# A conv, attention and expert block on one core: token loads two pieces ahead, delta products on VectorE, other ring sizes

## The chip, the cores and the metric

The kernel runs on one core of a Trainium2 chip. A core has five engines, each with its own queue that is worked in order: TensorE (PE, matmuls, results in PSUM), VectorE (DVE), ScalarE (ACT, activation functions), GpSimd (POOL) and SyncE (SP, here only for issuing DMAs). They meet through semaphores. All data comes from HBM by DMA into SBUF, 128 partitions wide. The metric is device time in microseconds (us) of one execution; lower is better.

## The reference

`x` is four images of 64 x 64 tokens with 128 channels, in float32. Layer 0 normalises each image in groups of 4 channels and adds the output of a selective-scan block; layer 1 adds an attention block and then an expert block, each on normalised tokens.

```python
x = x + _L0_conv_ref(_gn(x), ...)                 # scan block
t = _to_tokens(x)
t = t + _L1_attn_ref(_ln_t(t), ...)               # 16 heads of width 8
t = t + _L1_ffn_ref(_ln_t(t), ...)                # 64 experts, top 8 tokens for each
```

What matters here is the scan block. Each image's 4096 tokens are scanned in three orders: forward, backward, and in 16 interleaved slices. For each order:

```python
x = silu(causal_conv1d(x, conv_w, conv_b))                 # 256 rows, 4 taps
x_dbl = einsum('rd,bdl->brl', x_proj_w, x)                 # 8 rows of dt, 16 of B, 16 of C
delta = softplus(einsum('dr,brl->bdl', dt_w, dt_raw) + dt_b)
# for each token:  h = h * exp(delta * A) + (delta * u) * B ;  y = sum over 16 states of h * C
y = (y + D * x) * silu(z)
```

The three results are added and projected back to 128 channels.

## The kernel before

The program has an opening stage and three later ones. In the opening stage the scan inputs of all four images are made, and image 0 is scanned. Then comes a short stretch that prepares image 0 for the attention, then the attention loops of the four images with the scans of images 1 to 3 and other work running beside them, then the experts. The change touches the opening stage alone.

**Pieces and their order.** The code is written as Python generators. Each `yield` is a place where another generator may go on; the order in which instructions are recorded is the order in each engine's queue, and nothing reorders it afterwards. In `tile_kernel` (L1532 to L1541) two such streams are woven: `first` is the scan of image 0, `others` makes the inputs of all images. Each turn `others` takes 1.3 yields on average and `first` takes one. Within `others`, `flow` keeps two pieces active. So the number of yields in a piece decides how its instructions stand against the scan's.

**Inputs.** `norm` (L288) reads one image. In four pieces of 1024 tokens it loads tokens into `x_g` (512 KB, SP, one buffer), transposes them on PE in two halves of four 128 x 128 blocks, copies each half to `xn` (ACT, L308) and takes `bn_stats` of it (DVE, L311). The statistics are then combined over groups with two tiny matmuls, and `xn` is scaled in place (DVE, L332). `of_chunk` (L369) makes, for one image, order and chunk of 1024 tokens: the convolution on PE, `u` by silu on ACT, the projections, and `r` = delta by softplus on ACT (L431). `u`, `r` and the rows of B and C are stored to DRAM (SP). For "early" chunks, all 12 of image 0 and the first two of image 1, `of_chunk` also multiplies delta by u, in place in `u`, two products of 128 x 1024 (L440), and stores that as `d_du`; the very first chunk does so on DVE, the other 13 on POOL. The u that is overwritten must have been stored first. Later chunks get that product elsewhere, beside the attention. `gate` makes silu(z).

**Scan of image 0.** `of_image` (L475) with `alone=True` runs 384 steps: 3 orders, 4 chunks, 32 steps each. A step covers 16 rows times 8 states on 128 partitions and 1024 tokens. For each step:

- `load` (L501), four steps ahead: delta (SP queue) and du (ACT queue), 512 KB each for two steps, spread from DRAM over the partitions; three buffers of delta and four of du. At a chunk's start also the B and C rows, in two halves `q` (L487). Half 0 comes from a ring of three buffers in the pool `rows`, half 1 from two in the pool `lone`.
- `exp` (L521), three steps ahead: dA = exp(A delta) on ACT. The first step of a pair writes a tile of its own, the second overwrites delta.
- `inputs` (L530), one step ahead: dB = du x B on DVE (L537), written to PSUM.
- `step` (L539): the scan itself, one `tensor_tensor_scan` on DVE (L547); the chunk's last column is kept by a small POOL copy (`ends`, L549, not in an order's last chunk); then POOL multiplies h by C into `hC` (L554), a ring of five tiles.
- `sums`/`total`: PE adds up over the states (L585, `y`), for two steps at a time, one block of four steps later. This frees the tiles of `hC`.
- `out`: once per four steps DVE adds D u (L601), and SP stores the result.

So DVE's queue repeats scan, dB, scan, dB, with the occasional instruction of `others` behind a dB, and POOL's repeats ends, hC. In the very first chunk SP also issues 96 small loads of A (L231), once image 0's norm is recorded.

Of the kernel before, what the change touches and what calls it, by code (L numbers as in the profile page):

```python
# [11 lines left out]
F32 = mybir.dt.float32  # L12
# [4 lines left out]
P = 128  # L17
C = 128
# [8 lines left out]
T = 1024  # L27
# [184 lines left out]
def orders(b):  # L212

    return ORDERS[min(b, 1)]
# [20 lines left out]
class Inputs:  # L235
# [52 lines left out]
    def norm(self, b):  # L288

        nc = self.nc  # L290
        while b - 1 in self.gated and self.gated[b - 1] < NC:
            yield WAIT
        self.gated[b] = 0
        xin = self.x[b].rearrange("(t p) c -> p t c", p=P)
        xn = self.big.tile([P, L + 6], F32, tag="xn", name=f"xn_{b}")
        nc.gpsimd.memset(xn[:, 0:3], 0.0)
        nc.gpsimd.memset(xn[:, L + 3 :], 0.0)
        stats = self.small.tile([P, L // 512, 6], F32, tag="stats", name=f"stats_{b}")
        for g in range(NC):
            x_g = self.piece.tile([P, 8, C], F32, tag="x_g", name=f"x_{b}_{g}")  # L300
            nc.sync.dma_start(out=x_g, in_=xin[:, g * 8 : g * 8 + 8, :])
            yield
            for k in range(2):
                ps = yield from self.bank(f"xt_{b}_{g}_{k}")
                for i in range(4):
                    nc.tensor.transpose(ps[:, i * P : (i + 1) * P], x_g[:, 4 * k + i, :], self.ident)
                cut = xn[:, 3 + g * T + k * 512 : 3 + g * T + (k + 1) * 512]
                nc.scalar.copy(cut, ps)  # L308
                self.leave()
                yield  # L310
                nc.vector.bn_stats(stats[:, 2 * g + k, :], cut)  # L311
        mv = self.small.tile([P, 2], F32, tag="mv", name=f"mv_{b}")
        nc.vector.bn_aggr(mv, stats.rearrange("p g s -> p (g s)"))
        gm = self.small.tile([P, 4], F32, tag="gm", name=f"gms_{b}")
        ps = yield from self.bank(f"gm_{b}")
        nc.tensor.matmul(ps[:, 0:1], self.group, mv[:, 0:1], start=True, stop=True)
        yield
        nc.vector.tensor_copy(gm[:, 0:1], ps[:, 0:1])
        self.leave()
        nc.vector.tensor_sub(gm[:, 1:2], mv[:, 0:1], gm[:, 0:1])  # L320
        nc.vector.tensor_mul(gm[:, 1:2], gm[:, 1:2], gm[:, 1:2])
        nc.vector.tensor_add(gm[:, 1:2], gm[:, 1:2], mv[:, 1:2])
        ps = yield from self.bank(f"gv_{b}")
        nc.tensor.matmul(ps[:, 0:1], self.group, gm[:, 1:2], start=True, stop=True)
        yield
        nc.vector.tensor_copy(gm[:, 2:3], ps[:, 0:1])
        self.leave()
        rstd_of(nc, gm[:, 3:4], gm[:, 2:3], *self.cols)
        yield
        for g in range(NC):  # L330
            cut = xn[:, 3 + g * T : 3 + (g + 1) * T]
            nc.vector.tensor_scalar(cut, cut, gm[:, 0:1], gm[:, 3:4], ALU.subtract, ALU.mult)  # L332
        self.normed[b] = xn
# [35 lines left out]
    def of_chunk(self, b, order, c):  # L369
        while b not in self.normed or (order == 2 and b not in self.sliced):  # L370
            yield WAIT
        src = self.sliced[b] if order == 2 else self.normed[b]
        nc, w, key = self.nc, self.ws[order], f"{b}_{order}_{c}"
        made = {
            "delta": self.dram.tile([DI, T], F32, name=f"d_delta_{key}"),
            "du": self.dram.tile([DI, T], F32, name=f"d_du_{key}"),
            "u": self.dram.tile([DI, T], F32, name=f"d_u_{key}"),
            "bc": self.dram.tile([2, NS, T], F32, name=f"d_bc_{key}"),
        }

        def keep(name, t):
            nc.sync.dma_start(out=made[name].rearrange("(m p) t -> p m t", p=P), in_=t)

        def reads(k, g):

            at = c * T + g * 512
            if order == 1:
                end = L + 6 - at - k
                return src[:, end - 512 : end][:, ::-1]
            return src[:, at + k : at + k + 512]  # L390

        halves = [slice(g * 512, (g + 1) * 512) for g in range(T // 512)]
        u = self.piece.tile([P, 2, T], F32, tag="u", bufs=2, name=f"u_{key}")
        banks = yield from self.banks(4, f"cv_{key}")
        for m in range(2):
            for g in range(2):
                for k in range(4):
                    nc.tensor.matmul(  # L398
                        banks[2 * m + g], w["conv"][:, k, m * P : (m + 1) * P], reads(k, g), start=(k == 0), stop=(k == 3)
                    )  # L400
                yield
        yield
        for m in range(2):
            for g, cut in enumerate(halves):
                nc.scalar.activation(u[:, m, cut], banks[2 * m + g], AF.Silu, bias=w["conv_b"][:, m : m + 1])
                self.leave()
        yield
        xd = self.piece.tile([X_ROWS, T], F32, tag="xd", name=f"xds_{key}")
        for g, cut in enumerate(halves):
            ps = yield from self.bank(f"xd_{key}_{g}")  # L410
            for m in range(2):
                nc.tensor.matmul(ps[:X_ROWS], w["x"][:, m, :], u[:, m, cut], start=(m == 0), stop=(m == 1))  # L412
            yield
            nc.scalar.copy(xd[:, cut], ps[:X_ROWS])
            self.leave()
        keep("u", u)
        yield
        r = self.piece.tile([P, 2, T], F32, tag="r", name=f"r_{key}")
        banks = yield from self.banks(4, f"dt_{key}")
        for m in range(2):  # L420
            for g, cut in enumerate(halves):
                at = 32 * (2 * m + g)
                rows = slice(at, at + R)
                nc.tensor.matmul(banks[2 * m + g], w["dt"][rows, m, :], xd[rows, cut], start=True, stop=True)
        nc.sync.dma_start(out=made["bc"][0], in_=xd[B_ROW : B_ROW + NS])
        nc.sync.dma_start(out=made["bc"][1], in_=xd[C_ROW : C_ROW + NS])
        yield
        yield
        for m in range(2):
            for g, cut in enumerate(halves):  # L430
                nc.scalar.activation(  # L431
                    r[:, m, cut], banks[2 * m + g], AF.Softplus, bias=w["dt_proj_b"][:, m : m + 1]
                )
                self.leave()
        yield
        by_early = early(b, order, c)
        if by_early:
            by = nc.vector if (b, order, c) == (0, orders(0)[0], 0) else nc.gpsimd
            for m in range(2):
                by.tensor_mul(u[:, m, :], r[:, m, :], u[:, m, :])  # L440
        yield
        keep("delta", r)
        if by_early:
            yield
            keep("du", u)
        self.made[b, order, c] = made
        yield


class Scans:  # L450
# [24 lines left out]
    def of_image(self, b, made, alone=False):  # L475
# [10 lines left out]

        def rows_of(order, c, q):  # L487
            for i, name in enumerate(("B", "C")):
                if alone and q:
                    t = self.lone.tile([P, T], F32, tag=name, bufs=2, name=f"{name}{q}_{b}_{order}_{c}")  # L490
                else:
                    t = self.rows.tile([P, T], F32, tag=name, bufs=3, name=f"{name}{q}_{b}_{order}_{c}")
                src = made[b, order, c]["bc"][i, q * NS2 : (q + 1) * NS2]
                nc.sync.dma_start(out=t, in_=src.unsqueeze(0).to_broadcast([16, NS2, T]))
                spread[order, c, name, q] = t
            if q == 1:
                return
            if c < NC - 1:
                ends[order, c] = self.small.tile([P, NB], F32, tag="ends", name=f"ends_{b}_{order}_{c}")
# [39 lines left out]
        def step(s):  # L539
# [10 lines left out]
            if alone:  # L550
                if s + 1 < n:
                    inputs(s + 1)
                tiles["du", s] = self.lone.tile([P, T], F32, tag="hC", bufs=5, name=f"hC_{b}_{s}")
                nc.gpsimd.tensor_mul(tiles["du", s], h, spread[order, c, "C", j % 2])  # L554
                return
            if s + 1 < n:
# [951 lines left out]
def tile_kernel(tc, ctx, x, in_proj_w, dirs, out_proj_w, attn, gate, weight1, weight2, out):  # L1508
# [15 lines left out]
    with ExitStack() as fill:  # L1524
# [10 lines left out]
        with tc.manual_schedule():  # L1535
            first = Pace(decays(nc, dirs, ws, inputs), scans.of_image(0, inputs.made, True))
            others = Pace(flow(inputs.pieces(range(nb)), 2, 10))
            while not first.done:
                others.run(1.3)
                first.run(1.0)  # L1540
            others.rest()  # L1541
    bank = scans.bank = Bank(ctx.enter_context(tc.tile_pool(name="bank", bufs=1, space=PSUM)), 1)
# [115 lines left out]
```

## Time and profile before

The times of four runs are 11401.74 to 11427.02 us, median 11415.23 us. The profiled execution is one more:

| | |
|---|---|
| profiled execution, its own time | 11421.51 us |
| its span | 11419.8 us |
| granted TensorE clock, mean | 0.943 |
| busy: PE, DVE, ACT, POOL | 86%, 73%, 87%, 33% |
| first scan of image 0 starts | 107.0 us |
| last scan of image 0 ends | 1815.5 us |
| busy from 0 to 1816 us: PE, DVE, ACT, POOL | 1350, 1601, 1091, 1352 us |
| first exponential of the attention starts | 2061.1 us |
| last one starts | 11168.4 us |

How to read it: "busy" is the time in which an engine had an instruction at work. A row of the groups gives line, engine, operation, tiles out and in, their sizes and the count; then the busy time and the mean of one in ns; then the idle time of the engine just before them and what ended it. A row of a timeline gives start, duration, engine, line and operation, and in brackets the idle time before it with its releaser. The chain of waits is the work that ended last, followed back from the end.

### The profile page before, as it was taken

The numbers are of one execution on the slowest core, as the hardware profiler recorded it, in microseconds if no ns is written. First come the engines' busy times: TensorE is split into PE (matmuls) and PEld (weight loads), VectorE is DVE, ScalarE is ACT, GpSimd is POOL, SyncE is SP. The second block draws the span as 40 slices with busy tenths as digits, with TensorE's granted clock in tenths as the row PEclk, the third lists the DMA queues.
The fourth block names the chain that finished last, engine by engine and source line by source line (L and its number), as shares of the span: only waits on it lengthen the run. The fifth ranks groups of instructions, "written<-read, shape, count | busy, mean of one in ns | idle before, by whom it ended". The sixth has DMA issues, their size and how long they took to land.

```text
span 11419.8 us, 183032 instructions
## 1 busy us (share of the span) xinstructions
PE 9875.4 (86%) x68358; PEld 3271.3 (29%) x68358; DVE 8315.2 (73%) x8379; ACT 9990.0 (87%) x10828; POOL 3800.4 (33%) x3917
## 2 busy tenths in 40 slices
PE   6787782788988889899998898999998999999995
PEld 2233331222222222222222222222222223333323
DVE  7998897888988987999988979988999321111212
ACT  4566572899999999999999999999999999989992
POOL 5887674332323213424233224233332110000000
PEclk8898895899999999999999999999999999999997
DMA  6787796555565665655656755655556332222225
GB/s 191 226 243 227 216 245 191 161 147 152 148 155 152 179 170 153 157 152 141 154 145 160 193 155 154 158 144 146 146 150 164 116 100 72 76 71 84 75 65 186
DMA packets 900979, 1747.51 MB, mean 153 GB/s; under 512 B 203150, under 2 KB 443846, under 8 KB 899830
## 3 DMA queue, kind: packets, MB, share of 16 engines
q1 hardware_dynamic: 764734, 1469.68, 47.4%
q0 software_dynamic: 93856, 156.41, 4.9%
q10 hardware_dynamic: 41496, 109.71, 3.6%
q8 instruction: 537, 8.80, 0.3%
q14 instruction: 356, 2.92, 0.1%
HBM read 1379.76 MB, written 355.47 MB: 152 GB/s over the span
## 4 chain that ended last, share of the span: by engine, by line
PE 37%; ACT 23%; DVE 14%; issue 14%; DMA 9%; SPq 1%; POOL 1%; ACTq 0%; DVEq 0%; POOLq 0%
PE acc L998 21%; ACT e L989 19%; PE s L984 10%; DVE h L547 6%; DMA delta<-d_delta 3%; DVE dB L537 2%; DMA du<-d_du 2%; PE cv L398 1%; ACT dA L528 1%; PE y L585 1%; ACT delta L528 1%; PE fo L1155 1%; PE h L1142 1%; DMA x<-in_x_dram 1%; PE xd L412 1%
## 5 line engine op out<-in xcount | busy, mean ns | idle before, releaser
L989 ACT ACTIVATE e<-s 128x1024 f32<-128x1024 f32 x8192 | 7773.9, 1105 | 233.7 <-PE s L984 222.2
L998 PE MATMUL acc<-e,val 128*32 128x512 f32 x32768 | 5253.7, 616 | 105.8 <-ACT av L1007 93.1
L984 PE MATMUL s<-qm,key 32*128 32x512 f32 x16384 | 2646.9, 501 | 591.6 <-ACT e L989 559.9
L984 PEld LDWEIGHTS s<-qm,key 32*128 32x128 f32 x16384 | 1012.1, 184 | 4451.9 <-issue 2495.1
L549 POOL COPY ends<-h 128x1 f32<-128x1 f32 x1152 | 1284.3, 1116 | 2282.3 <-DVE h L547 2274.8
L537 DVE TENSOR_TENSOR dB<-du,B 128x1024 f32<-128x1024 f32 x960 | 1301.1, 1355 | 428.9 <-PE y L585 224.7
L998 PEld LDWEIGHTS acc<-e,val 128*32 128x32 f32 x32768 | 971.6, 109 | 1606.5 <-issue 789.0
L547 DVE TENSOR_TENSOR_SCAN h<-dA,ends,dB 128x1024 f32<-128x1024 f32 x576 | 1350.4, 2344 | 101.7 <-ACT dA L528 59.0
L528 ACT ACTIVATE dA<-delta,A 128x1024 f32<-128x1024 f32 x768 | 935.6, 1218 | 462.0 <-DMA delta<-d_delta 429.2
L547 DVE TENSOR_TENSOR_SCAN h<-delta,ends,du 128x1024 f32<-128x1024 f32 x432 | 1012.3, 2343 | 126.0 <-ACT delta L528 64.0
L554 POOL TENSOR_TENSOR hC<-h,C 128x1024 f32<-128x1024 f32 x384 | 985.4, 2567 | 209.4 <-PE y L585 108.8
L528 ACT ACTIVATE delta<-delta,A 128x1024 f32<-128x1024 f32 x768 | 936.9, 1220 | 6.3 <-ACT dA L528 0.8
L558 DVE TENSOR_TENSOR du<-h,C 128x1024 f32<-128x1024 f32 x576 | 701.1, 1217 | 0.1
L558 DVE TENSOR_TENSOR dB<-h,C 128x1024 f32<-128x1024 f32 x576 | 701.0, 1217 | 0.0
L537 DVE TENSOR_TENSOR du<-du,B 128x1024 f32<-128x1024 f32 x576 | 690.5, 1199 | 4.5 <-DMA B<-d_bc 4.4
L1013 POOL DMA_DIRECT2D d_ctx<-av x512 | 260.2, 518 | 1015.3 <-DVE av L1007 645.8
L398 PE MATMUL cv<-xn,conv 128*128 128x512 f32 x1024 | 478.8, 622 | 38.1 <-DVE xn L332 25.8
L579 POOL DMA_DIRECT2D d_du<-x_delta x272 | 157.2, 578 | 1015.4 <-DVE x_delta L578 954.7
L547 DVE TENSOR_TENSOR_SCAN h<-dA,dB 128x1024 f32<-128x1024 f32 x192 | 438.8, 2285 | 43.4 <-ACT dA L528 32.4
L585 PE MATMUL y<-dB,sel 128*32 128x256 f32 x4608 | 376.8, 399 | 7.6 <-DVE xT L1182 5.0
L547 DVE TENSOR_TENSOR_SCAN h<-delta,du 128x1024 f32<-128x1024 f32 x144 | 328.9, 2284 | 67.4 <-issue 34.6
L585 PE MATMUL y<-du,sel 128*32 128x256 f32 x4608 | 361.9, 386 | 0.0
(246 smaller groups left out, 7115.5 us busy)
## 6 DMA issues: line engine op xcount, KB each, us to landing
delta<-d_delta SPq DMA_DIRECT2D x768, 512.0 KB
du<-d_du SPq DMA_DIRECT2D x576, 512.0 KB
du<-d_du ACTq DMA_DIRECT2D x192, 512.0 KB
key<-d_q SPq DMA_DIRECT2D x352, 256.0 KB
d_u<-u SPq DMA_DIRECT2D x48, 1024.0 KB
d_delta<-r SPq DMA_DIRECT2D x48, 1024.0 KB
B<-d_bc SPq DMA_DIRECT2D x96, 512.0 KB
C<-d_bc SPq DMA_DIRECT2D x96, 512.0 KB
```

Source lines behind the costliest of these rows:

```text
L398: nc.tensor.matmul(banks[2 * m + g], w["conv"][:, k, m * P : (m + 1) * P], reads(k, g), start=(k == 0), stop=(k == 3))
L528: nc.scalar.activation(tiles["delta", s], t, AF.Exp, scale=A)
L537: nc.vector.tensor_mul(tiles["du", s], du, spread[order, c, "B", j % 2])
L547: nc.vector.tensor_tensor_scan(h, dA, dB, first, ALU.mult, ALU.add)
L549: nc.gpsimd.tensor_copy(ends[order, c][:, at : at + 1], h[:, T - 1 :])
L554: nc.gpsimd.tensor_mul(tiles["du", s], h, spread[order, c, "C", j % 2])
L558: nc.vector.tensor_mul(dB, h, spread[order, c, "C", j % 2])
L585: nc.tensor.matmul(y[32 * g : 32 * g + 32, : T // 4], self.sel[:, j // 2, :], hC[:, 256 * g : 256 * g + 256], start=(j == 0), stop=(j == 3),)
L984: nc.tensor.matmul(s_ps[:, k, :], keys[f"{i // 4}"][rows, cut].bitcast(F32R), queries[j, qb][rows, :].bitcast(F32R), start=True, stop=True,)
L989: nc.scalar.activation(e, s_ps, AF.Exp, scale=1.0 / math.sqrt(D))
L998: nc.tensor.matmul(accs[j, qb][32 * k : 32 * k + 32, :], v[:, k * VW : k * VW + 32], es[i][k // 2][:, k % 2, :], start=(kc == 0), stop=(kc ...
L1013: nc.gpsimd.dma_start(out=self.context[b][h * D : h * D + D, cut], in_=av[32 * k : 32 * k + D, :])
```

## The change

There are five edits, all in the opening stage.

1. `norm`: `x_g` gets two buffers. The first two loads are recorded at once, with six yields after them (one for image 0); the load of piece g + 2 is recorded after piece g. Each `bn_stats` is recorded after the copy two halves later, with a yield of its own; the last two follow at the end.
2. `of_chunk`: the delta products of all early chunks are recorded on DVE, each with a yield behind it.
3. `rows_of`: for image 0, three of every four tiles of B and of C come from `rows`, and each fourth (half 1 of an odd chunk) from `lone`, where one tile is left of each.
4. `step`: `hC` has six tiles.
5. `tile_kernel`: `others` takes 1.4 yields a turn.

The second `x_g` buffer and the sixth `hC` tile take 4 KB of each partition, each; the two dropped tiles of B and C give back 8 KB.

```diff
@@ norm
+        def bring(g):
+            x_g = self.piece.tile([P, 8, C], F32, tag="x_g", bufs=2, name=f"x_{b}_{g}")
+            nc.sync.dma_start(out=x_g, in_=xin[:, g * 8 : g * 8 + 8, :])
+            return x_g
+
+        coming, made = [bring(0), bring(1)], []
+        for _ in range(6 if b else 1):
+            yield
         for g in range(NC):
-            x_g = self.piece.tile([P, 8, C], F32, tag="x_g", name=f"x_{b}_{g}")
-            nc.sync.dma_start(out=x_g, in_=xin[:, g * 8 : g * 8 + 8, :])
-            yield
+            x_g = coming[g]
             for k in range(2):
...
                 nc.scalar.copy(cut, ps)
                 self.leave()
+                made.append(cut)
                 yield
-                nc.vector.bn_stats(stats[:, 2 * g + k, :], cut)
+                if len(made) > 2:
+                    nc.vector.bn_stats(stats[:, len(made) - 3, :], made[-3])
+                    yield
+            if g + 2 < NC:
+                coming.append(bring(g + 2))
+        for i in range(len(made) - 2, len(made)):
+            nc.vector.bn_stats(stats[:, i, :], made[i])
+            yield
@@ of_chunk
         if by_early:
-            by = nc.vector if (b, order, c) == (0, orders(0)[0], 0) else nc.gpsimd
             for m in range(2):
-                by.tensor_mul(u[:, m, :], r[:, m, :], u[:, m, :])
+                nc.vector.tensor_mul(u[:, m, :], r[:, m, :], u[:, m, :])
+                yield
@@ rows_of
-                if alone and q:
-                    t = self.lone.tile([P, T], F32, tag=name, bufs=2, name=...)
+                if alone and 2 * (c % 2) + q == 3:
+                    t = self.lone.tile([P, T], F32, tag=name, name=...)
@@ step
-                tiles["du", s] = self.lone.tile([P, T], F32, tag="hC", bufs=5, name=f"hC_{b}_{s}")
+                tiles["du", s] = self.lone.tile([P, T], F32, tag="hC", bufs=6, name=f"hC_{b}_{s}")
@@ tile_kernel
-                others.run(1.3)
+                others.run(1.4)
```

More of the change, by code (lines that the diff above doesn't have):

```diff
@@ L488, in rows_of @@
             for i, name in enumerate(("B", "C")):
-                if alone and q:
-                    t = self.lone.tile([P, T], F32, tag=name, bufs=2, name=f"{name}{q}_{b}_{order}_{c}")
+                if alone and 2 * (c % 2) + q == 3:
+                    t = self.lone.tile([P, T], F32, tag=name, name=f"{name}{q}_{b}_{order}_{c}")
                 else:
```

## Prediction

> **What bounds the kernel now.** I read the page's slices first (where is which engine full), then the groups of instructions and the waits of the first 1816 us, then the timelines of VectorE and GpSimd there. Slices:
>
> ```profile
> PE   6787782788988889899998898999998999999995
> DVE  7998897888988987999988979988999321111212
> ACT  4566572899999999999999999999999999989992
> POOL 5887674332323213424233224233332110000000
> ```
>
> A slice is 285 us. In the first six, DVE and POOL are full and ACT is not; afterwards ACT and PE are (attention). Everything the change touches lies in the opening stage: the scan of image 0 ends at 1815.5 us, and the attention opens only on its stored result. Later instructions are the same on every engine, so what the opening gains or loses passes on whole. Its groups on DVE, from the first scan on:
>
> ```profile
> L537 DVE TENSOR_TENSOR dB<-du,B 128x1024 f32<-128x1024 f32 x383 | 604.4, 1578 | 23.5 <-DMA du<-d_du 9.5 <-DMA B<-d_bc 1.2
> L547 DVE TENSOR_TENSOR_SCAN h<-dA,ends,dB 128x1024 f32<-128x1024 f32 x144 | 337.8, 2346 | 20.9 <-ACT dA L528 3.8
> L311 DVE BATCH_NORM_STATS2 stats<-xn 128x6 f32<-128x512 f32 x24 | 16.6, 691 | 52.1 <-ACT xn L308 52.0
> ...
> L440 POOL TENSOR_TENSOR u<-r,u 128x1024 f32<-128x1024 f32 x26 | 72.4, 2805 | 8.6 <-ACT r L431 8.6
> ```
>
> Two things are to be seen. DVE's one large wait is that of the statistics for ScalarE's copy: 52.0 us. And dB takes 1578 ns in the mean, where an undisturbed one takes 1.23 us. The timelines say why:
>
> ```profile
> 326.94 5.59 POOL L440 TENSOR_TENSOR u<-r,u 128x1024 f32<-128x1024 f32 x2 [0.51 <-ACT r L431]
> 332.48 1.18 POOL L549 COPY ends<-h 128x1 f32<-128x1 f32 x1
> 333.62 2.36 POOL L554 TENSOR_TENSOR hC<-h,C 128x1024 f32<-128x1024 f32 x1
> ...
> 328.13 2.35 DVE L547 TENSOR_TENSOR_SCAN h<-dA,ends,dB 128x1024 f32<-128x1024 f32 x1
> 330.51 3.11 DVE L537 TENSOR_TENSOR dB<-du,B 128x1024 f32<-128x1024 f32 x1
> 333.75 2.35 DVE L547 TENSOR_TENSOR_SCAN h<-delta,ends,dB 128x1024 f32<-128x1024 f32 x1
> 336.13 3.38 DVE L537 TENSOR_TENSOR dB<-du,B 128x1024 f32<-128x1024 f32 x1
> ```
>
> A scan and a POOL product run side by side, but a product of DVE and one of POOL exclude each other: dB, begun at 330.51 while POOL works, ends with POOL's u. In phase, hC hides under the scan (2.35 beside 2.35 us) and dB costs 1.23; whatever delays POOL pushes hC onto the next dB, at up to 2.2 us each. Summed over the opening's dBs, what exceeds 1.24 us is 132 us. Going back on POOL from each: 54 us (28 dBs) follow an L440 product, 75 us (50 dBs) an hC that waited for its buffer, thus for PE's y (POOL's waits: "PE y L585" 108.8 us, and six at the start of a chunk, 58.9 us, put down to "issue", where y was late too). Such a wait:
>
> ```profile
> 1117.86 2.48 POOL L554 TENSOR_TENSOR hC<-h,C 128x1024 f32<-128x1024 f32 x1 [3.44 <-PE y L585]
> ...
> 1120.65 3.23 DVE L537 TENSOR_TENSOR dB<-du,B 128x1024 f32<-128x1024 f32 x1
> ```
>
> **The change part by part**
>
> *Start of image 0: -11 us.* With one x_g buffer the four loads go in turn; image 0's statistics wait 4.8 us before each later piece and the last ends at 53.2 us. With two buffers, pieces 0 and 1 are there when PE becomes free at 30.8; loads 2 and 3 are issued at about 32.5 and 33.5 instead of 39 and 45.5, and land 4.3 us later (their length in the chain), with both and the A loads in flight perhaps 6: the last statistics end near 42. SP, which issues 96 small A loads (37 us) behind the last x load and only then lets the first u out (82.76), also comes 11-12 us earlier, so neither holds the other back. Bounds: 0 (x_1, now ahead of the dt weights on SP, delays weight work that ends at 30.8) and -16.9 (all of image 0's waits of the statistics).
>
> *Norms of images 1 to 3: -39 us.* The waits are 20.3, 16.8 and 14.9 us (at 465, 890 and 1300 us): a bn_stats stands right behind its copy, the copy behind a transpose, that behind a load that waited for the only buffer. Now the first two loads go out some two scan steps (8 us) ahead, the third and fourth about three steps before their copies, and each bn_stats stands two copies later. ScalarE's exp leads the scan by a median of 7 to 8 us, so a copy that waits 1 to 3 us for its load is mostly absorbed there; what would be late next is exp, and the scan behind it. I leave a quarter of the 52. Bounds -52 and 0. SP gains nothing in issues (16 loads of 0.38 us either way) but waits less in front of delta loads: it stood 36.8 us for "PE xt" and 35.8 us for earlier x loads.
>
> *Six tiles for hC, ring of four for B and C: -44 us.* y is summed for two steps at a time, one block later, so with five tiles step 4k+5 reuses the tile of step 4k, whose y is issued in that same step: no slack. With six the tightest reuse has one step, 3.7 us. Most of POOL's gaps for y are 0.8 to 3.6 us and vanish; eight of 4.0 to 6.4 leave 0.3 to 2.7 (together 9 us), the six at chunk starts (6.5 to 12.9) leave about 22. 75 - 31 = 44. Bounds 0 and -75. B and C cost nothing: in either ring a tile is reloaded when its chunk of two before has ended, four steps ahead of need.
>
> *Delta products on DVE: +45 us.* Off: the 54 us above. On: 26 products of 1.18 us (the pair that DVE does already takes 2.36): 30.7. The wait: each product stands in DVE's queue for r, the softplus on ScalarE, one yield behind it, while ScalarE issues one or two steps ahead of DVE. For each of the 13 chunks I took from the trace the end of the exp ahead of its softplus plus 1.28 (table load) and 1.24 (two halves), and the end of the dB before the product: 2.2, 2.1, 6.1, 4.8, 3.7, 4.8, 0.9, 5.0, 9.3, 0, 4.4, 0.6, 0: 44 us. Behind the waiting product stands the scan, and behind that delta's buffers, so ScalarE cannot run ahead meanwhile. In numbers, chunk (1,2): DVE would come to the product at 292.9, when ScalarE has this still ahead of it:
>
> ```profile
> 294.01 1.15 ACT L528 ACTIVATE dA<-delta,A 128x1024 f32<-128x1024 f32 x1 [1.43 <-DMA delta<-d_delta]
> 295.17 1.28 ACT L431 ACT_TABLE_LOAD   x1
> 296.47 0.69 ACT L431 ACTIVATE r<-dt,dt_proj_b 128x512 f32<-128x512 f32 x1
> ```
>
> Last, the port: what follows a dB at once and needs two SBUF streams loses its turn to the waiting ends copy and hC. Three of three first xn scalings (L332) show it: 2.97 us for 0.80, +2.17:
>
> ```profile
> 530.08 5.14 DVE L332 TENSOR_SCALAR xn<-xn,gms 128x1024 f32<-128x1024 f32 x4
> ...
> 530.17 2.33 POOL L554 TENSOR_TENSOR hC<-h,C 128x1024 f32<-128x1024 f32 x1
> ```
>
> A first product that waits longer hides this; the six that wait less pay 7.4 more. In eight chunks the new yield puts the second product behind the next dB: 8 x 2.17 = 17.4. Sum 30.7 + 44 + 7.4 + 17.4 - 54 = +45. Bounds: -23 (no waits, no lost turns) and +90 (waits twice as long). A delta product also waits for the store of u that it overwrites (26.9 us in image 0's first chunk, where SP is behind the A loads); no later one on POOL did, so I take nothing.
>
> The Trainium skill (Perfetto Trace Analysis, Optimizing Scalar/DVE Operations) says that because the two engines share a read port, moving work between them might not help. By that rule alone this part would be 0 and the whole sum -84 instead of -39; the rows above decide, since they price DVE's new wait for r, of which the rule says nothing.
>
> *Pace 1.4: 0.* Yields grow by 10 or 5 per norm and 2 in each of 14 chunks, 63 on some 880 (7%), the rate by 7.7%; the last softplus comes 4 steps later of 384, with 19 steps of plain scanning left to cover it.
>
> *Returned: +10.* Three delta pairs circulate: a load is issued when a scan frees its buffer, its exp starts 7 to 13 us later, and is used five scans after the issue. Shorter steps shorten that lead. DVE's waits for exp, du and B are 39 us now; a quarter more is 10 (bounds 0 and +39).
>
> Sum: -11 - 39 - 44 + 45 + 10 = -39 us. The profiled execution took 11421.5 us (span 11419.8), 6.3 above the median of 11415.2, an ordinary run; against the median this gives **11376 us**.
>
> **Rivals**
>
> *Slower: the wait for r.* One mechanism, in the 13 early chunks (110 to 600 us). Against it stand exps that end before the scan needs them; for it stand ScalarE's waits for delta (298.1 us in 63 waits), which come ahead of softplus in its queue. Without the waits the sum is -39 - 44 = -83. It decides once they total 83 us, 6.4 a chunk (two of the 13 estimates are near or above that); at 106 us, 8.2 a chunk (the largest estimate is 9.3), the time is 11415 + 23 = 11438.
>
> *Nothing from the norms.* The copies still stand in ScalarE's queue: if the loads stay late, exp is late and the scan waits where bn_stats did. 11376 + 39 = 11415. For it: one copy waited 15.2 us for its transpose; against it: the load now leaves two to three steps ahead.
>
> *hC keeps colliding.* If PE's y is late by more than a step, the sixth tile moves the gap by one step and no more: 11376 + 44 = 11420. For it: the chunk-start gaps of up to 12.9 us; against it: 3.6 us or less in most.
>
> *Delta products free.* If DVE finds r ready and POOL's order does not shift, that part is -23 to 0: 11308 to 11331. For it: three estimates near 0.
>
> **How the numbers follow.** The median of four runs spreads 25 us, so less than 0.2% (23 us) can't be told from no change. Forecast (11345 to 11392) 0.42; delta products free, below 11345, 0.22; nothing from the norms or from hC, 11392 to 11438, 0.18; slower 0.18. Faster by over 0.2%: 0.64. Eight in ten: 11295 (all gains near their bounds) to 11445 (slower case, its nearer half).
>
> **What would show it.** Right: the scan of image 0 ends near 1776 instead of 1815.5; "stats <- ACT xn" falls from 52 to some 13 us after the start; the first scan begins near 96 instead of 107; dB's mean goes from 1578 towards 1330 ns; POOL's "PE y" waits halve; and a new DVE wait "u <- ACT r" of some 44 us appears, with u's mean near 2.1 us instead of 1.18. Wrong: if that wait exceeds 100 us, if the wait of the statistics returns as "h <- ACT delta", or if the attention, from 1815 us on, does not just shift.

## The result, and the profile after

The changed kernel takes 11402.05 us (median of 34 runs) against 11412.03 us for the kernel before (52 runs): a ratio of 0.9991, with an interval of 0.9987 to 0.9996. That is 10 us, or 0.09%: clear of zero, but below the 0.2% under which the prediction counted no change. The forecast was 11376 us; its range of 11295 to 11445 holds the result.

The profiled execution has a span of 11399.4 us (own time 11401.1 us), 20.4 less than before's 11419.8. First DVE's and POOL's slices of the page after, as shown for before:

```profile
DVE  6889898888888987999988979988998221111212
POOL 5778784332323212424233124233331110000000
```

The picture is the old one: in the first six slices DVE and POOL are both full. DVE stands a tenth lower in the first three; POOL stands a tenth lower in the second and third, and a tenth higher in the three after them. The groups of VectorE from the first scan to the last scan of image 0, after (busy us, mean ns, idle us ahead):

```profile
L551 DVE TENSOR_TENSOR dB<-du,B 128x1024 f32<-128x1024 f32 x384 | 517.0, 1346 | 40.5 <-DMA du<-d_du 23.2 <-DMA B<-d_bc 4.8
L453 DVE TENSOR_TENSOR u<-r,u 128x1024 f32<-128x1024 f32 x26 | 37.8, 1468 | 57.9 <-ACT r L445 40.0 <-DMA du<-d_du 14.6 <-DMA d_u<-u 3.3
```

dB fell from 1578 to 1346 ns, as foretold (1330). In its place stands a new group, the delta products: 37.8 us of work and 57.9 us of waiting. VectorE's waits, in us, times and the longest, first after, then before:

```profile
DVE h L561 <- ACT dA L542: 23.8, 21, 3.2
DVE dB L551 <- DMA du<-d_du: 23.2, 13, 6.9
DVE h L561 <- ACT delta L542: 20.5, 15, 2.5
DVE stats L319 <- ACT xn L314: 19.1, 4, 9.6
```

```profile
DVE dB L537 <- DMA du<-d_du: 16.3, 6, 6.8
DVE h L547 <- ACT delta L528: 13.1, 6, 2.6
DVE h L547 <- ACT dA L528: 8.7, 9, 2.4
```

The statistics wait 19.1 us instead of 52.0, but the scan now waits 44.3 us for its exponentials instead of 21.8, and dB 23.2 for du instead of 16.3 (some 7 us of either lie ahead of the first scan).

The traces of this study were cut in the same way. "Excess" is what the dBs take beyond 1.24 us each; "other waits" is all idle time of VectorE between the first and the last scan of image 0 that is not the statistics' or the delta products'. In us, from one profiled execution of each kernel:

| kernel | first scan | last scan ends | excess of dB | products: work + wait | statistics wait | other waits | first exp of attention, after last scan |
|---|---|---|---|---|---|---|---|
| before | 107.0 | 1815.5 | 131.5 | on POOL | 52.1 | 85.3 | 245.6 |
| after | 98.5 | 1808.4 | 43.4 | 38.2 + 57.9 | 19.1 | 116.3 | 242.4 |
| e1_products_pool | 99.5 | 1777.8 | 94.1 | on POOL | 19.9 | 126.7 | 242.8 |
| e2_products_alone | 107.4 | 1819.6 | 63.7 | 47.3 + 34.5 | 59.5 | 74.3 | 244.4 |
| e3_norm_alone | 99.2 | 1739.1 | 123.1 | on POOL | 13.2 | 74.6 | 251.5 |
| e4_six_alone | 108.0 | 1809.1 | 94.2 | on POOL | 54.7 | 112.6 | 245.9 |
| e5_pace13 | 99.3 | 1779.8 | 33.1 | 41.4 + 54.6 | 19.5 | 100.8 | 275.2 |
| e6_products_later | 98.4 | 1765.5 | 48.5 | 49.4 + 14.2 | 12.6 | 108.8 | 244.2 |
| e7_delta4 | 99.4 | 1745.0 | 134.5 | on POOL | 13.8 | 68.4 | 251.1 |
| e8_norm_six | 99.1 | 1723.7 | 94.3 | on POOL | 14.8 | 86.4 | 252.7 |
| e9_norm_pace14 | 99.5 | 1799.3 | 164.3 | on POOL | 6.2 | 94.3 | 243.8 |
| e10_norm_products | 98.6 | 1744.3 | 73.1 | 48.2 + 13.1 | 10.8 | 74.1 | 250.6 |
| e11_norm_products_six | 99.7 | 1726.4 | 37.0 | 49.1 + 11.1 | 13.1 | 89.9 | 253.2 |
| e12_norm_pace135 | 99.9 | 1755.4 | 135.1 | on POOL | 12.2 | 72.6 | 244.0 |

From before to after the scan of image 0 ends 7.1 us earlier: start -8.5, excess -88.1, products +96.1, statistics -33.0, other waits +31.0, the rest -4.6. Of the 20.4 us of the span, 12.4 lie in the attention loops (first to last exponential: 9108.4 and 9096.0 us). All fourteen traces here have 9096 to 9119 us there with the same instructions, so that part is put down to the spread of single executions (the 52 runs of before span 33 us); the runs say 10 us.

### The profile page after: what moved, and what is told of

Same layout as the page of the kernel before. It is cut to its first block, busy times and chain, and to the rows that moved or that the text cites. A ratio compares the mean times of both kernels' runs of the same rounds, so it can differ in the third digit from the quotient of the medians.

```text
span 11399.4 us, 183033 instructions
## 1 busy us (share of the span) xinstructions
PE 9874.8 (87%) x68358; PEld 3271.9 (29%) x68358; DVE 8259.6 (72%) x8405; ACT 9988.6 (88%) x10828; POOL 3744.8 (33%) x3891
## 4 chain that ended last, share of the span: by engine, by line
PE 37%; ACT 24%; issue 14%; DVE 13%; DMA 10%; POOL 1%; SPq 1%; ACTq 0%; DVEq 0%; POOLq 0%
PE acc L1012 21%; ACT e L1003 20%; PE s L998 10%; DVE h L561 6%; DMA delta<-d_delta 4%; PE cv L412 2%; DVE dB L551 2%; DMA du<-d_du 1%; ACT dA L542 1%; ACT delta L542 1%; PE y L599 1%; PE fo L1169 1%; PE h L1156 1%; PE xd L426 1%; DVE du L572 1%
## 5 line engine op out<-in xcount | busy, mean ns | idle before, releaser
L551 DVE TENSOR_TENSOR dB<-du,B 128x1024 f32<-128x1024 f32 x960 | 1212.6, 1263 | 422.2 <-PE y L599 219.1
L568 POOL TENSOR_TENSOR hC<-h,C 128x1024 f32<-128x1024 f32 x384 | 993.4, 2587 | 166.1 <-PE y L599 85.9
L599 PE MATMUL y<-hC,sel 128*32 128x256 f32 x3072 | 246.4, 454 | 166.1 <-DVE o L615 154.0
```

The costliest lines, as they stand in the source:

```text
L551: nc.vector.tensor_mul(tiles["du", s], du, spread[order, c, "B", j % 2])
L599: nc.tensor.matmul(y[32 * g : 32 * g + 32, : T // 4], self.sel[:, j // 2, :], hC[:, 256 * g : 256 * g + 256], start=(j == 0), stop=(j == 3),)
```

## The experiments

**First: each part by itself, and the pace.** The theory was the sum of the prediction: gains at the norms and the six tiles, a price for the delta products behind the softplus, nothing for the pace. The main rival was that removed waits come back as other waits. e1 to e4 ran on one chip beside the kernel before (median there 11424.49 us). e5, e6, e7 and e9 ran on a second (11423.73 us), e8, e10, e11 and e12 on a third (11420.42 us). So kernels are compared by their ratios.

*e1_products_pool* is the change with the products back on POOL, its two yields kept.

```diff
-                nc.vector.tensor_mul(u[:, m, :], r[:, m, :], u[:, m, :])
+                by.tensor_mul(u[:, m, :], r[:, m, :], u[:, m, :])
```

> The changed kernel with the delta products of the 13 early chunks back on POOL (their yields stay). Theory 'price on DVE': in the changed kernel the 26 products cost DVE 38 us of work and 58 us of waits in front of them, against 54 us of collisions that they caused on POOL. Taking them off DVE then gives 96 - 54 = 42 us, less some 15 us that shorter steps give back as waits for exp: about 11375 us, with the wait 'u <- ACT r' gone from DVE, dB's excess back from 43 to about 95 us, and the scan stretch (first to last scan of image 0) near 1680 us instead of 1710. Rival 'the move pays': the collisions come back in full, with those by late y in chunks 0 to 3 (68 us in the kernel before): 11440 us or more. Rival 'floor': the loop of delta loads bounds the opening, so that what DVE gains comes back as waits for exp: 11395 to 11410 us.

Measured: 11381.83 us, 0.9961 (0.9948 to 0.9973). The products' move costs the changed kernel 0.30%, some 34 us, near what the theory said; in the traces the scan of image 0 ends 30.6 us later with them on DVE. The prediction said +45.

*e2_products_alone* is the kernel before with only the products moved to DVE, with their yields, at pace 1.3.

```diff
-                by.tensor_mul(u[:, m, :], r[:, m, :], u[:, m, :])
+                nc.vector.tensor_mul(u[:, m, :], r[:, m, :], u[:, m, :])
+                yield
```

> The kernel before with the delta products on DVE and their yields, and nothing else of the change (pace 1.3, one x_g buffer, five hC tiles). Theory 'price on DVE': +42 us, 11454 us, slower than before by 0.3 to 0.5%. Rival 'the move pays': 11412 us or less. Rival 'floor': the waits for r lie beside waits for exp that are there anyway: 11405 to 11425 us.

Measured: 11424.71 us, 0.9999 (0.9990 to 1.0008). Not as the theory had it: here the move is free to within 10 us. dB's mean falls to 1399 ns, and against that stands the new wait (VectorE's waits):

```profile
DVE u L439 <- ACT r L431: 34.4, 8, 7.3
```

The excess falls by 67.8 us where 54 were taken to go, and the wait is 34.4 us where 44 were taken; work and wait are 81.8 us. The statistics wait 7.4 us longer, and other waits are 11.0 us shorter. The time is the one that the rival 'floor' named (11405 to 11425 us); its reason, that the waits for r lie beside waits that are there anyway, holds for those 11 us. So the price of the move isn't one number. That it depends on how far ScalarE is behind when DVE reaches the product is argued here; e6 tests it.

*e3_norm_alone* has the norm part alone: two `x_g` buffers, loads ahead, later statistics. Room for the buffer comes from the ring of B and C, which has the change's form; `hC` has five tiles, the products are on POOL, the pace is 1.3.

```diff
+        coming, made = [bring(0), bring(1)], []
...
+                    nc.vector.bn_stats(stats[:, len(made) - 3, :], made[-3])
...
+                if alone and 2 * (c % 2) + q == 3:
```

> The kernel before with the two x_g buffers, the early loads and the late statistics (the ring of four for B and C makes the room), products on POOL, five hC tiles, pace 1.3. Theory: -8 us at the start and -33 us in three norms, 11371 us; the wait of the statistics after the first scan falls from 52 to about 19 us. Rival 'floor': 11395 us or more, with 'h <- ACT' up by what the statistics lose.

Measured: 11359.21 us, 0.9943 (0.9930 to 0.9955), a gain of 65 us: more than the expectation, and more than six times that of the whole change. VectorE's waits there: the statistics stand at 13.2 us, as the prediction had it, and nothing came back: the scan's waits for exponentials (10.0 us, and 3.2 for those that overwrite delta) are together below the 21.8 us of before.

```profile
DVE stats L319 <- ACT xn L314: 13.2, 3, 7.5
DVE h L561 <- ACT dA L542: 10.0, 8, 2.5
```

One thing goes with this part unasked: its yields (10 or 5 a norm, 35 in all) slow the pieces. Their last gate matmul ends when the scan is at step 383 of 384; before it was step 361. No run separates that from the loads and the statistics, nor the ring of B and C from either; e9 and e12 bear on it.

*e4_six_alone* is the kernel before with the six tiles and the other ring of B and C.

```diff
-                tiles["du", s] = self.lone.tile([P, T], F32, tag="hC", bufs=5, name=f"hC_{b}_{s}")
+                tiles["du", s] = self.lone.tile([P, T], F32, tag="hC", bufs=6, name=f"hC_{b}_{s}")
```

> The kernel before with six hC tiles and the ring of four for B and C, nothing else. Theory: the dB excess that late y caused, 75 us, falls to about 31 us, so -44 us, less 10 to 15 us of waits for exp: about 11380 us. Rival 'floor': 11400 us or more, with dB's excess down and the waits for exp and du up by nearly as much. Rival 'y is late by more than a step': dB's excess hardly falls, 11410 us.

Measured: 11416.01 us, 0.9991 (0.9983 to 1.0000). POOL's waits for y halve and the excess falls by 37.3 us, near the 44 of the prediction. But 27.3 us come back as other waits of DVE, above all for exponentials (24.6 us and, for those that overwrite delta, 15.3). From the waits of POOL and of VectorE (before, POOL's were 108.8 us and this one of VectorE's 8.7):

```profile
POOL hC L554 <- PE y L585: 58.0, 24, 6.7
```

```profile
DVE h L547 <- ACT dA L528: 24.6, 17, 3.2
```

Here the rival holds: POOL no longer holds DVE up, and DVE then meets the next late thing. Of the 37.3 us, 29.3 lie in the last eight chunks of the scan, and so does all that came back. Whether one late moment of PE and ScalarE had delayed both is not shown.

*e5_pace13* is the change at the old pace.

```diff
-                others.run(1.4)
+                others.run(1.3)
```

> The changed kernel with the pace of 1.3 instead of 1.4. What is left open by the first four runs: six hC tiles took 37 us of dB excess away and got 27 us of waits for exp and du back; the changed kernel has 116 us of them, the two norms alone at pace 1.3 only 75. Theory 'pace': 1.4 puts 7.7% more of the other pieces' work into ScalarE's queue per scan step, ahead of the exps; at 1.3 those waits fall from 116 towards 85 us, and 20 to 30 us are gained in the scan, less what the inputs cost that then remain when the scan ends (63 yields more at the old pace: some 9 steps' worth of pieces after the last scan, 5 to 20 us): 11375 to 11395 us. Theory 'tiles': the waits for exp come from shorter steps, the pace does nothing: 11400 us or, with the remainder, 11410.

Measured: 11416.99 us, 0.9996 (0.9987 to 1.0004). The scan of image 0 ends 28.6 us earlier, as theory 'pace' had it, but the first exponential of the attention stands 275.2 us behind it instead of 242.4: the last gate matmul of the pieces ends at 1805.1 us, 25 us after the scan. This remainder had been put at 5 to 20 us; it is 33 us and takes back all that the scan gained, so the time is not the one expected. With the added yields in the pieces, 1.3 is too slow to finish them; 1.4 finishes them, and costs the scan as much.

**Second: where the loss of the change lies.** The parts alone add up to 0.57% + 0.09% + 0.01%, some 76 us, and together they gave 10.

*e6_products_later* is the change with the delta products two yields later, behind the store of delta; the number of yields is kept.

```diff
+        yield
+        keep("delta", r)
         if by_early:
+            yield
             for m in range(2):
                 nc.vector.tensor_mul(u[:, m, :], r[:, m, :], u[:, m, :])
                 yield
-        yield
-        keep("delta", r)
-        if by_early:
-            yield
             keep("du", u)
```

> The changed kernel with the two delta products recorded two yields later (after the store of delta, the number of yields is the same). Theory 'price on DVE': the wait in front of the products, 58 us, is due to their place right behind softplus; 2.7 us later in DVE's order each of 13 first products waits about 2.7 us less: 58 falls to about 25 us, time about 11375 us. Rival: the wait only turns into a later wait for exp, since ScalarE is what is behind: 11400 us.

Measured: 11374.51 us, 0.9957 (0.9945 to 0.9970): 0.34% better than the change, as the theory had it. The wait for the softplus falls from 57.9 to 14.2 us (groups of VectorE):

```profile
L456 DVE TENSOR_TENSOR u<-r,u 128x1024 f32<-128x1024 f32 x26 | 49.2, 1900 | 14.2 <-ACT r L445 14.2
```

The mean of a product rises from 1468 to 1900 ns: 11 of the 26 now take over 1.3 us, where 4 did, so POOL's work passes less often during DVE's wait. This isolates the price of the place: the same products on the same engine, two yields apart. Only the store of delta moves besides, two yields ahead.

*e7_delta4* asks whether late exponentials come from the three buffers of delta. It is e3 with a fourth one.

```diff
+                if alone and name == "delta" and s // 2 % 4 == 3:
+                    t = self.lone.tile([P, T], F32, tag="delta", name=f"{name}_{b}_{s}")
+                else:
+                    t = self.deep.tile([P, T], F32, tag=name, bufs=bufs, name=f"{name}_{b}_{s}")
```

> The kernel with the norm part alone (11359 us) plus a fourth buffer of delta for image 0. Theory 'delta loop': the waits for exp come from a load that can only be issued when a scan frees its buffer; with four buffers the load goes up to two steps earlier, ScalarE's waits for delta (about 300 us) fall by a third or more, and DVE's waits for exp and du fall from 75 to about 50 us: 11330 to 11345 us. Rival 'ScalarE's queue': exp is late because it stands behind copies and silu that wait for PE, or SP is held up by its other issues; then nothing changes: 11355 to 11365 us.

Measured: 11360.49 us, 0.9944 (0.9932 to 0.9957), the same as e3 and what the rival named. ScalarE's waits for delta are still 353.7 us (380.6 in e3; a third less was expected), and DVE's other waits 68.4 us (74.6). So the loop of delta's buffers, which stood behind the prediction's "returned" waits, is not what holds this schedule. With six tiles, or in the changed kernel, a fourth buffer was not tried.

*e8_norm_six* is e3 with six tiles of `hC` (the edit of e4).

> Norm part (11359 us) and six hC tiles with the ring of four, pace 1.3, products on POOL. Theory 'given back': as on the kernel before, six tiles take some 37 us of dB excess off and waits for exp and du return most of it: 11345 to 11360 us. Theory 'pace': with the norms' stalls gone and the slow pace, the six tiles' gain stays: about 11325 us.

Measured: 11336.75 us, 0.9926 (0.9913 to 0.9938). This lies between the two expectations. The six tiles bring 0.17% more here, 0.09% in e4: against e3 the excess falls by 28.8 us, and 11.8 us of other waits come back. The intervals of e3 and e8 overlap a little; the scan of image 0 ends 15.4 us earlier in the trace.

*e9_norm_pace14* is e3 at pace 1.4.

```diff
-                others.run(1.3)
+                others.run(1.4)
```

> The kernel with the norm part alone (11359 us at pace 1.3), at pace 1.4. Theory 'pace': 20 to 30 us slower, 11380 to 11390 us, with DVE's waits for exp and du up from 75 to 100 us or more. Theory 'tiles': 11355 to 11362 us.

Measured: 11402.59 us, 0.9983 (0.9974 to 0.9992). Against e3 the pace costs 0.40%, in the profiled spans 52 us (11400.5 and 11348.7), more than was expected. POOL's waits for y rise, and with them dB. First e3, then e9, the waits of POOL and the groups of VectorE:

```profile
POOL hC L568 <- PE y L599: 129.2, 46, 9.7
```

```profile
POOL hC L568 <- PE y L599: 177.3, 53, 8.6
```

```profile
L551 DVE TENSOR_TENSOR dB<-du,B 128x1024 f32<-128x1024 f32 x384 | 597.1, 1555 | 26.5 <-DMA du<-d_du 10.5 <-DMA B<-d_bc 3.0
```

```profile
L551 DVE TENSOR_TENSOR dB<-du,B 128x1024 f32<-128x1024 f32 x384 | 638.4, 1663 | 27.2 <-DMA du<-d_du 7.9 <-DMA B<-d_bc 6.3
```

PE's sums for the scan stand behind matmuls of the pieces: in the 3 us ahead of each hC that starts late (63 of them in e9), PE is busy for 98% of the time, 70% with the pieces and 28% with sums. So hC waits for its tile, and is pushed onto dB. The excess rises by 41 us and other waits by 20. The first four chunks of the scan, beside which the early chunks of `of_chunk` are made, take 566.5 us in e3 and 568.9 in e9; the other eight take 1073.4 and 1130.9. The products are on POOL and add no yields in either, so all pieces are packed closer by the same share; why only the later chunks pay is not shown.

**Third: the parts without their prices.** If the losses are the place of the products and the pace, a version with the products behind delta's store, no yields of their own and pace 1.3 keeps the gains.

*e10_norm_products* is e3 with the products so placed.

```diff
         keep("delta", r)
         if by_early:
+            for m in range(2):
+                nc.vector.tensor_mul(u[:, m, :], r[:, m, :], u[:, m, :])
             yield
             keep("du", u)
```

> Norm part (11359 us) with the delta products on DVE, recorded behind the store of delta without a yield of their own, so that the number of yields is that of the norm part alone; five hC tiles, pace 1.3. Theory: their waits shrink to about 15 us, their work is 31 us, 13 lost turns cost up to 28 us, and 60 us of dB excess go: 11345 to 11360 us. If the products cost what they cost in the changed kernel (96 us against 51): 11400 us.

Measured: 11347.19 us, 0.9937 (0.9925 to 0.9950), as the theory had it.

*e11_norm_products_six* is e10 with six tiles of `hC`.

> The same with six hC tiles: the whole change except for the pace of 1.4, the yields of the products and their place. If the parts add up: norm -65, products -10, six tiles -8: about 11335 us. If six tiles give everything back: as without them. If they hurt together as in the changed kernel: 11380 us or more.

Measured: 11334.95 us, 0.9920 (0.9906 to 0.9934). Here the parts add up, to the 11335 us expected. This is the best of the study, 0.8% faster than the kernel before and 0.7% faster than the changed one, though not to be told from e8. Its rows on VectorE:

```profile
L455 DVE TENSOR_TENSOR u<-r,u 128x1024 f32<-128x1024 f32 x26 | 48.1, 1889 | 11.1 <-ACT r L445 9.5 <-DMA d_u<-u 1.4 <-ACT delta L540 0.2
L549 DVE TENSOR_TENSOR dB<-du,B 128x1024 f32<-128x1024 f32 x384 | 510.5, 1330 | 31.0 <-DMA du<-d_du 14.1 <-DMA B<-d_bc 4.1
```

Between e6 and e11 only the products' own yields, a yield ahead of them and the pace differ: 0.37%, some 40 us. The first four chunks of the scan, beside which all products are made, take 567.4 and 559.4 us, the other eight 1099.7 and 1067.3. So four fifths of what is left of the change's loss lie where no product is, which points to the pace again: the pieces end at step 365 of the scan in e6 and at step 383 in e11.

*e12_norm_pace135* is e3 at 1.35.

> The norm part alone at a pace of 1.35 (1.3: 11359 us, 1.4: 11403). Theory 'pace': late y and late exp grow with the work packed into each step, so it lies between, 11375 to 11390 us. Rival 'alignment': the loss at 1.4 is a matter of where single pieces fall against the scan, and 1.35 can be anything from 11350 to 11410.

Measured: 11357.27 us, 0.9944 (0.9930 to 0.9957): not as theory 'pace' had it, since a time between those of 1.3 and 1.4 was expected. The scan of image 0 does end in between (1739.1, 1755.4 and 1799.3 us for 1.3, 1.35 and 1.4), but the first exponential follows 251.5, 244.0 and 243.8 us after it: at 1.3 the last gate matmul ends 5 us before the scan, at 1.35 63 us before. So the time is flat from 1.3 to 1.35 and rises by 1.4. From 1.35 to 1.4 the pieces are not even done sooner (1692.2 and 1688.7 us); only the scan has got less far by then (steps 369 and 356). With three rates the rival 'alignment' is not ruled out.

For the norm part this says that its gain does not hang on the slow pieces of e3: here they end at step 369, near the 361 of before, and the gain is the same.

## Why the prediction was right or wrong

**The range held, the size of the gain did not.** Most of the chance stood on faster by over 0.2%; what came is within 0.2%. The time lies where the prediction put "nothing from the norms or from hC" (11392 to 11438), but that is not what happened: the statistics' waits fell by 33 us and the excess by 88. That the range held owes something to luck, for the errors have both signs: the norm part alone gives more than was summed, and the pace, put at nothing, costs. By terms, from the traces before and after:

| step of the prediction | predicted, us | measured, us |
|---|---|---|
| start of image 0 | -11 | -8.5 |
| norms of images 1 to 3 | -39 | -33.0 |
| excess of dB: products off POOL and six tiles (54 + 44) | -98 | -88.1 |
| products on DVE: work and lost turns (30.7 + 7.4 + 17.4) | +55.5 | +38.2 |
| products: wait for r | +44 | +57.9 |
| returned as waits | +10 | +31.0 |
| the rest of the scan of image 0 | 0 | -4.6 |
| sum, to the end of the scan of image 0 | -39 | -7.1 |

**Right.** The first scan starts at 98.5 us (96 was named), dB's mean is 1346 ns (1330), a new wait for the softplus stands on DVE, and behind the scan the same instructions follow. Other signs missed: the scan of image 0 ends at 1808.4 us (1776), the statistics wait 19.1 us (13), and a delta product takes 1.47 us (2.1). The wait can be read at the place that the prediction chose, chunk (1,2). In the timelines of ScalarE and VectorE after:

```profile
298.46 1.15 ACT L542 ACTIVATE dA<-delta,A 128x1024 f32<-128x1024 f32 x1 [1.34 <-DMA delta<-d_delta]
299.62 1.28 ACT L445 ACT_TABLE_LOAD   x1
300.92 0.69 ACT L445 ACTIVATE r<-dt,dt_proj_b 128x512 f32<-128x512 f32 x1
...
294.47 1.23 DVE L551 TENSOR_TENSOR dB<-du,B 128x1024 f32<-128x1024 f32 x1
302.21 1.22 DVE L453 TENSOR_TENSOR u<-r,u 128x1024 f32<-128x1024 f32 x1 [6.51 <-ACT r L445]
```

DVE is done with dB at 295.7 and stands 6.51 us, while ScalarE still waits for a delta load, does an exp, loads the table and makes half of the softplus. The estimate for this chunk from the old trace was 4.8 us (exp to 295.16, 2.52 more for table and half a softplus, DVE free at 292.9). Of the 57.9 us, 40.0 are put down to r. The other two large waits (6.42 us at 259.23, 8.15 at 593.48) are put down to a load of du, but both products start 1.30 us after the first part of a softplus, as the second of its four parts ends, which is their half of r. So they too are waits for r, which makes 54.6.

**Mis-sized: "Returned: +10".** 31 us came back as waits for exp and du. The price was worked out from delta's three buffers. On the norm part alone a fourth buffer changed nothing (e7), but there little was returned: other waits are 74.6 us in e3 against 85.3 before. The six tiles return 27.3 of 37.3 us in e4, 11.8 of 28.8 in e8 and 15.8 of 36.1 in e11 (against e10). And the pace adds 20 in e9. With all the parts at pace 1.3 and no yields for the products, e11 has 89.9 us of other waits, 4.6 more than before; so most of the 31 us goes with the pace, the yields and the products' place, and not with shorter steps. What exactly makes exp late after the tiles came free stays open.

**Wrong: "Pace 1.4: 0".** The argument was one of averages: yields grow by 7%, the rate by 7.7%, so the pieces stay where they were. They did: they end at step 365 instead of 361, with 19 steps left, as was said. The step that failed is from there to a price of nothing. The added yields lie in the early chunks and the norms, and the rate holds for all, so where no yields were added the pieces' PE and ScalarE work is packed closer beside the scan. On the norm part alone 1.4 costs 0.40%, some 46 us (e9), and the -65 of the norm part shrinks to -19. At 1.35 it costs nothing (e12), so the loss doesn't grow evenly with the rate, and why it has set in by 1.4 stays open. In the full change the old pace isn't better (e5, 0.9996 against 0.9991), since the 63 added yields then leave pieces behind the scan. So pace and yields are one price, to be taken together: e6 against e11 has it at 40 us.

**"Delta products on DVE: +45".** 34 us on the chip (e1), so the size is about right, in this place of the queue. There is luck in it: the terms were read from the trace of before, and on that kernel the move costs nothing (e2). The lost turns were too many: of the eight second products behind a next dB, one paid, and seven took 1.22 us. In the rival "the wait for r" the mechanism was named rightly, but its point of decision, 83 us, wasn't reached. The rival "delta products free" has the number of e2, though not its condition, since DVE waits 34.4 us for r there; its condition is nearer in e10 and e11, with another place (13.1 and 11.1 us of wait): e10 stands 0.06% below e3 and e11 0.06% below e8, both inside their intervals. The Trainium skill (Perfetto Trace Analysis, Optimizing Scalar/DVE Operations) states that moving work between the two engines might not help, as they share a port; e2, e10 and e11 agree with it. Where in the new queue the work is put decided more here: 0.34%, some 39 us, between the change and e6.

**"Six tiles: -44".** The excess fell by nearly that, yet the time by 0.09 to 0.17% (10 to 20 us: e4, e8 against e3, e11 against e10). The named sign, that POOL's waits for y halve from 108.8 us, came in e4 (58.0 us) and in e11 (58.5), but not in the changed kernel (85.9; 66.5 in e5, so the pace is part of it). With the waits put down to "issue", which the prediction counted among them at the chunks' starts, it did come: 89.5 us against 167.7.

**Not foreseen: the norm part's size.** It was -50 with the start; alone, with its yields at pace 1.3, it gave -65. In the trace that is -7.8 at the start, -38.9 at the statistics, -8.4 of excess, -10.7 of other waits and -10.6 in smaller things (the scalings of xn alone went from 15.4 to 11.1 us), with 5.9 more behind the scan. That part of the prediction was nearly its sum; the other -30 us are shorter collisions and waits elsewhere, which were not looked for.

## What to carry to other kernels

An instruction that is moved to another engine costs its work plus what it waits for in the new queue, less what it no longer disturbs; put it behind the point where its input is surely there, and here two places later were worth 39 us. Where work of two streams is woven by a rate, the rate and every added turn are part of the change: look at where the turns were added, not at their sum, and try more than one rate: here 1.3 and 1.35 did equally well with the norm part, and 1.4 lost 0.40%. When a collision is removed, ask whether what was late on one side is also late on the other; 27 of 37 us came back in e4, 16 of 36 in e11.

## What the runs showed of the hardware

A product of DVE that follows dB at once doesn't always lose its turn to POOL. In the changed kernel it goes with which POOL instruction already stands in line. First a product behind POOL's small copy, then one behind POOL's product, in the timelines after:

```profile
305.73 1.23 DVE L551 TENSOR_TENSOR dB<-du,B 128x1024 f32<-128x1024 f32 x1
305.76 1.24 POOL L563 COPY ends<-h 128x1 f32<-128x1 f32 x1 [7.70 <-DVE h L561]
306.87 1.22 DVE L453 TENSOR_TENSOR u<-r,u 128x1024 f32<-128x1024 f32 x1
306.96 3.34 POOL L568 TENSOR_TENSOR hC<-h,C 128x1024 f32<-128x1024 f32 x1
...
597.10 3.34 POOL L568 TENSOR_TENSOR hC<-h,C 128x1024 f32<-128x1024 f32 x1 [6.12 <-DVE h L561]
598.13 3.39 DVE L453 TENSOR_TENSOR u<-r,u 128x1024 f32<-128x1024 f32 x1
```

At 305.76 the copy waits out dB; the product begins at 306.87, ahead of hC, takes its 1.22 us, and hC pays the 1.0 (3.34 instead of 2.33). At 597.10, at the end of an order, there is no copy and hC is in line already: the product comes later and takes 3.39. All seven second products that had the copy in line took 1.22 us, with 3.33 to 3.37 us for the hC behind; this is the one that had not. The Trainium skill (SBUF — State Buffer, SBUF: two separate sides) has it that whichever of the two starts first holds the pair for its whole instruction; these rows agree, with the order of arrival read off the starts.
